# Layer 0's second product as two column tiles of 64 output rows each, in a two-layer graph attention kernel

## The chip, the cores and the metric

The kernel runs on one core of a Trainium2 chip. The metric is device time in microseconds (us) for one launch, which covers the whole computation for all 16 graphs. A core has a matrix engine (TensorE, PE in the profile; its weight loads are listed apart as PEld), VectorE (DVE), ScalarE (ACT), GpSimd (POOL) and queues that issue transfers (SP among them). The engines run beside each other and wait for each other's results.

## The reference, cut to what matters

Each of 16 graphs has 1024 nodes with 128 features, and a dense 0/1 adjacency matrix of 1024 x 1024. Everything is float32. Layer 0 is an attention layer with gates:

```python
h = jnp.einsum('bnf,df->bnd', x, Ww) + Wb
e = jnp.einsum('bjl,bkl->bjk', jnp.einsum('bjd,dl->bjl', h, A), h)
e = e + jnp.swapaxes(e, 1, 2)
scores = jnp.where(adj > 0, e, 0.0)
attention = jax.nn.softmax(scores, axis=1) * adj
h_prime = jax.nn.relu(jnp.einsum('bij,bjk->bik', attention, h))
...
return oc * jnp.tanh(ic * h_prime + fc * x)
```

Its output is added to x and normalised. Layer 1 has four heads, each with the two products `scores = h A h^T` and `tanh(adj * scores) @ h`; the heads' mean is added to its input and normalised again. The change concerns the product `attention @ h` of layer 0, which gives `h_prime`.

## The kernel before

Graphs are handled one after the other. For one graph the 1024 nodes are split into NB = 8 blocks of 128, and a row of 1024 results into NH = 2 ranges of 512 columns, the width of one matmul. The adjacency is held transposed, eight tiles of 128 x 1024 for a graph.

Layer 0 is a Python generator, `layer0(b)`. For each block j, `front(j)` makes the scores of block j against all nodes (line 232, two products into PSUM tiles `sc`), adds a bias and masks them on VectorE (line 235), takes the row maximum (line 240) and the exponential on ScalarE (line 242). `middle(j)` folds the softmax's denominator into the features, `hz = h / z` (lines 250 and 252), and multiplies by the adjacency (line 253). `back(j)` then adds the block's share to the accumulator `acc`: two products, one for each range of 512 columns, with `hz` (128 nodes x 128 features) as the stationary operand and `s` (128 nodes x 512) as the moving one (line 259). The accumulator is 128 features x 1024 nodes of PSUM and gathers the eight blocks; after the last one ScalarE turns it into `hpT` (line 276), which line 283 transposes for the gates.

In `layer0`, a step runs `front(i)`, yields, then runs `middle(i - 1)` and `back(i - 2)` and yields again, so a block is summed two steps after its scores.

The order of the work is written out by hand, and each engine runs its instructions in that order. The main loop at the end goes over 32 steps for a graph (4 heads x 8 blocks). A step issues `layer1_step`: the scores of one head and block (line 355, two products), their masking on VectorE (line 358) and tanh on ScalarE (line 362), and the second product of the step before the last (line 369, two products into layer 1's accumulator, lines 364 to 372). After that it advances the generator of the next graph's layer 0 by one piece. So a call of `back` stands in TensorE's order behind a pair of products of line 369 and before the next step's pair of line 355, or before line 175 (a head's projection) where one falls due. Layer 0 of the first graph has no layer 1 to run beside and runs ahead of the loop, with the preparation of the heads' weights (lines 114 to 131 and 141 to 147) between its pieces.

PSUM holds four shared tiles (`bank`) and the two accumulators `acc0` and `acc1`, which take the other half.

Of the kernel before, what the change touches and what calls it, by code (L numbers as in the profile page):

```python
# [22 lines left out]
def two_layer_adjacency_kernel(  # L23
# [26 lines left out]
    nc = tc.nc  # L50
    B, N, D = x.shape
    H = conv_w.shape[0]
    assert D == P and N % 512 == 0 and H % 2 == 0
    NB = N // P
# [143 lines left out]
    def layer0(b):  # L198
# [26 lines left out]
        acc = ps_acc.tile([P, N], F32, tag="acc0", name=f"acc0_{b}")  # L225
# [30 lines left out]
        def back(j):  # L256
            s, hz = steps.pop(j)
            for q in range(NH):
                nc.tensor.matmul(  # L259
                    acc[:, ts(q, 512)], hz, s[:, ts(q, 512)],  # L260
                    start=(j == 0), stop=(j == NB - 1),
                )

        for i in range(NB + 1):
            if i < NB:
                front(i)
                yield
            if i:
                middle(i - 1)
            if i > 1:  # L270
                back(i - 2)
            yield
        back(NB - 1)
        hpT = sb.tile([P, N], F32, tag="hpT", name=f"hpT_{b}", bufs=1)
        for q in range(NH):
# [209 lines left out]
```

## Time and profile before

| | us |
|---|---|
| median of the 2 runs shown | 2652.52 (2650.65 to 2654.38) |
| the profiled execution | 2653.64 |
| its span, first to last instruction | 2651.9 |
| TensorE busy | 2568.2 |
| VectorE busy | 1761.2 |
| ScalarE busy | 884.7 |
| GpSimd busy | 454.7 |

The profile is one execution, with times from the start of its span. A line of a group gives the source line, the engine and operation, the tiles written and read, the shape, and the count; behind it stand the busy time and the mean length of one in ns, and then the time for which the engine stood idle before such an instruction and what ended that. Matmuls overlap each other at their ends, so their mean length is longer than the step from one start to the next. In the slices, the span is cut into 40 equal parts and a digit is the busy share in tenths. A timeline line gives the start, the length, the engine, the instruction and how many were merged. The chain of waits follows the work back from the last instruction, at each step to whatever released it.

### The profile page before, as it was taken

What the parts mean: (1) busy time and instruction counts of PE and PEld (TensorE: products, weight loads), DVE (VectorE), ACT (ScalarE), POOL (GpSimd) and SP (SyncE); (2) the same over time, 40 slices, a digit from 0 to 9 for tenths busy, and PEclk for the clock granted to TensorE, in tenths of its full rate; (3) what the DMA queues carried; (4) which work ended last, traced back from release to release, by engine and by line L of the source; (5) the groups of instructions that cost most, each with busy time, mean ns of one, the idle gap of its engine ahead of it and who ended that gap; (6) DMA issues with size and microseconds to landing.
All of it is one profiled execution on the core that took longest, in us unless ns stands there. A gap on an engine that the chain in (4) does not pass through costs nothing.

```text
span 2651.9 us, 19837 instructions
## 1 busy us (share of the span) xinstructions
PE 2568.2 (97%) x6766; PEld 1229.0 (46%) x6766; DVE 1761.2 (66%) x3407; ACT 884.7 (33%) x1078; POOL 454.7 (17%) x200
## 2 busy tenths in 40 slices
PE   5699999999999999999999999999999999999997
PEld 3344444444444444444444444444444444444443
DVE  4566756767667576766767667576666767667554
ACT  1233333333333333333333333333333333333332
POOL 3121201212020121201212021121101212021000
PEclk7799999999999999999999999999999999999999
DMA  2202001020110102001020020101001020020000
GB/s 94 79 0 79 9 16 64 9 79 9 44 44 16 64 8 72 16 16 64 8 80 8 18 70 16 64 9 63 25 16 64 9 79 8 16 69 2 1 8 8
DMA packets 43526, 94.54 MB, mean 36 GB/s; under 512 B 4641, under 2 KB 22945, under 8 KB 43425
## 3 DMA queue, kind: packets, MB, share of 16 engines
q1 hardware_dynamic: 41120, 84.89, 9.1%
q0 software_dynamic: 2304, 8.39, 1.1%
q8 instruction: 53, 0.87, 0.1%
q14 instruction: 49, 0.39, 0.0%
HBM read 84.87 MB, written 8.39 MB: 35 GB/s over the span
## 4 chain that ended last, share of the span: by engine, by line
PE 90%; DVE 7%; issue 1%; ACT 1%; DMA 0%; SPq 0%; POOL 0%; POOLq 0%; ACTq 0%
PE acc L369 30%; PE sc L355 30%; PE acc L259 8%; PE sc L232 8%; PE pg L175 5%; PE pr L340 4%; DVE u L311 1%; DVE u L303 1%; DVE s L358 1%; PE pt L283 1%; PE pr L217 1%; DVE st L158 1%; DVE sum L381 1%; PE pt L393 1%; ACT x1T L327 0%
## 5 line engine op out<-in xcount | busy, mean ns | idle before, releaser
L358 DVE SCALAR_TENSOR_TENSOR s<-sc,h,adj 128x512 f32<-128x512 f32 x1024 | 746.3, 747 | 494.6 <-PE sc L355 472.3
L369 PE MATMUL acc<-s,h 128*128 128x512 f32 x2048 | 963.1, 593 | 14.7 <-DVE sum L381 14.7
L355 PE MATMUL sc<-x1T,g 128*128 128x512 f32 x2048 | 962.2, 592 | 0.0
L362 ACT ACTIVATE s<-s 128x1024 f32<-128x1024 f32 x512 | 541.1, 1057 | 1112.2 <-DVE s L358 1007.8
L369 PEld LDWEIGHTS acc<-s,h 128*128 128x128 f32 x2048 | 387.7, 190 | 509.5 <-issue 479.3
L355 PEld LDWEIGHTS sc<-x1T,g 128*128 128x128 f32 x2048 | 386.7, 190 | 434.8 <-issue 341.3
L207 POOL TENSOR_SCALAR mask<-adj 128x1024 bf16<-128x1024 f32 x128 | 354.4, 2780 | 364.3 <-DVE s L235 208.1
L242 ACT ACTIVATE s<-s,nmax 128x1024 f32<-128x1024 f32 x128 | 147.0, 1149 | 489.7 <-DVE nmax L240 472.1
L235 DVE SCALAR_TENSOR_TENSOR s<-sc,h,mask 128x512 f32<-128x512 f32 x256 | 186.0, 746 | 115.2 <-PE sc L232 101.8
L259 PE MATMUL acc<-s,hz 128*128 128x512 f32 x512 | 247.5, 607 | 2.3 <-DVE s L253 2.3
L232 PE MATMUL sc<-xT,gT 128*128 128x512 f32 x512 | 242.2, 596 | 0.0
L163 POOL TENSOR_TENSOR rs<-rs,mhalf 128x8 f32<-128x8 f32 x32 | 53.3, 1664 | 924.7 <-DVE rs L162 924.7
L299 POOL TENSOR_TENSOR u<-x,gate 128x1024 f32<-128x1024 f32 x16 | 30.5, 1908 | 863.3 <-DVE gate L297 808.1
L253 DVE TENSOR_TENSOR s<-s,adj 128x1024 f32<-128x1024 f32 x128 | 167.8, 1311 | 0.0
L240 DVE TENSOR_REDUCE nmax<-s 128x1 f32<-128x1024 f32 x128 | 156.2, 1220 | 4.4
L259 PEld LDWEIGHTS acc<-s,hz 128*128 128x128 f32 x512 | 99.0, 195 | 125.8 <-issue 117.7
L343 DVE TENSOR_TENSOR h<-pr,row_b 128x258 f32<-128x258 f32 x256 | 106.1, 425 | 74.1 <-PE pr L340 73.1
L232 PEld LDWEIGHTS sc<-xT,gT 128*128 128x128 f32 x512 | 97.4, 193 | 118.2 <-issue 113.1
L340 PE MATMUL pr<-row_w,x1T 128*128 128x258 f32 x512 | 127.7, 383 | 0.0
L175 PE MATMUL pg<-x1T,mT 128*128 128x512 f32 x256 | 123.6, 606 | 3.6 <-ACT x1T L327 3.6
L340 PEld LDWEIGHTS pr<-row_w,x1T 128*128 128x128 f32 x512 | 98.0, 191 | 55.1 <-issue 45.8
L176 ACT ACTIVATE g<-pg,tcol 128x512 f32<-128x512 f32 x128 | 87.8, 686 | 49.1 <-PE pg L175 46.8
(69 smaller groups left out, 909.8 us busy)
## 6 DMA issues: line engine op xcount, KB each, us to landing
adj<-in_adjT_dram SPq DMA_DIRECT2D x128, 512.0 KB, 4.4
xT<-in_xT_dram SPq DMA_DIRECT2D x16, 512.0 KB, 3.6
x<-in_x_dram SPq DMA_DIRECT2D x16, 512.0 KB, 4.0
out_dram<-y POOLq DMA_DIRECT2D x16, 512.0 KB, 3.9
row_w<-in_L_gnn_conv_w_dram SPq DMA_DIRECT2D x4, 64.0 KB, 2.9
wm<-in_L_gnn_attn_w_dram SPq DMA_DIRECT2D x4, 64.0 KB, 2.6
row_b<-in_L_gnn_conv_b_dram SPq DMA_DIRECT2D x4, 64.0 KB, 3.2
ct<-in_L_gnn_Ww_dram SPq DMA_DIRECT2D x1, 64.0 KB, 1.8
```

The costliest lines, as they stand in the source:

```text
L175: nc.tensor.matmul(pg, mT[i], src[:, ts(q, 512)], start=True, stop=True)
L207: nc.gpsimd.tensor_scalar(t, adj_t[b][j], 0.0, None, ALU.is_gt)
L232: nc.tensor.matmul(sc, gT[:, ts(j, P)], xTb[:, ts(q, 512)], start=True, stop=True)
L235: nc.vector.scalar_tensor_tensor(s[:, ts(q, 512)], sc, h[:, j, D : D + 1], masks[j][:, ts(q, 512)], op0=ALU.add, op1=ALU.mult,)
L240: nc.vector.tensor_reduce(nmax, s, AX.X, ALU.max, negate=True)
L253: nc.vector.tensor_mul(s, s, adj_t[b][j])
L259: nc.tensor.matmul(acc[:, ts(q, 512)], hz, s[:, ts(q, 512)], start=(j == 0), stop=(j == NB - 1),)
L340: nc.tensor.matmul(pr[:, :W1], x1T_t[b][:, ts(k, P)], row_w1[:, p, :], start=True, stop=True)
L355: nc.tensor.matmul(sc, g[:, ts(m, P)], x1T_t[b][:, ts(q, 512)], start=True, stop=True)
L358: nc.vector.scalar_tensor_tensor(s[:, ts(q, 512)], sc, rows[:, m, 2 * D + r : 2 * D + r + 1], adj[:, ts(q, 512)], op0=ALU.add, op1=ALU.mult,)
L362: nc.scalar.activation(s, s, AF.Tanh)
L369: nc.tensor.matmul(acc[:, ts(q, 512)], rows[:, m, ts(r, D)], s[:, ts(q, 512)], start=(m == 0), stop=(m == NB - 1),)
```

## The change

Each product of `back` is issued as two products. The first takes columns 0 to 63 of `hz` as the stationary operand and writes rows (partitions) 0 to 63 of `acc`; the second takes columns 64 to 127 and writes rows 64 to 127. Both read the same 512 columns of `s` whole. The sum over the eight blocks, the flags that open and close it, and every other line stay as they are. Line 232 and layer 1 still use the full width of the array.

```diff
         def back(j):
             s, hz = steps.pop(j)
             for q in range(NH):
-                nc.tensor.matmul(
-                    acc[:, ts(q, 512)], hz, s[:, ts(q, 512)],
-                    start=(j == 0), stop=(j == NB - 1),
-                )
+                for half in (slice(0, D // 2), slice(D // 2, D)):
+                    nc.tensor.matmul(
+                        acc[half, ts(q, 512)], hz[:, half], s[:, ts(q, 512)],
+                        start=(j == 0), stop=(j == NB - 1),
+                    )
```

## The prediction

> **What bounds the kernel now.** I read the page's busy times and slices first, then its chain of waits, the groups of section 5, and last the timeline and the chain around one call of the edited function.
>
> ```profile
> PE 2568.2 (97%) x6766; PEld 1229.0 (46%) x6766; DVE 1761.2 (66%) x3407; ACT 884.7 (33%) x1078; POOL 454.7 (17%) x200
> ...
> PE   5699999999999999999999999999999999999997
> ...
> PE 90%; DVE 7%; issue 1%; ACT 1%; DMA 0%; SPq 0%; POOL 0%; POOLq 0%; ACTq 0%
> ...
> L259 PE MATMUL acc<-s,hz 128*128 128x512 f32 x512 | 247.5, 607 | 2.3 <-DVE s L253 2.3
> ...
> L259 PEld LDWEIGHTS acc<-s,hz 128*128 128x128 f32 x512 | 99.0, 195 | 125.8 <-issue 117.7
> ```
>
> TensorE is full from the third slice to the last but one, and 90% of the chain is TensorE's: what is added there is added to the time. L259, the edited line, waited 2.3 us in all, so there is no slack to put work into. The code asks for 16 batches x 8 blocks x 2 column ranges = 256 products there and the row counts 512: each float32 product is two weight loads and two matmuls ("passes" below).
>
> A busy matmul may hide its true rate, so I take that from the chain of waits about 1.48 ms in:
>
> ```profile
> 1481.79 1.72 PE acc L259 x4
> 1483.51 1.72 PE sc L355 x4
> 1485.23 1.72 PE acc L369 x4
> 1486.94 1.72 PE sc L232 x4
> 1488.66 1.72 PE sc L355 x4
> ```
>
> and the timeline of TensorE:
>
> ```profile
> 1500.51 1.88 PE L369 MATMUL acc<-s,h 128*128 128x512 f32 x4
> 1502.23 1.88 PE L259 MATMUL acc<-s,hz 128*128 128x512 f32 x4
> 1503.95 1.88 PE L175 MATMUL pg<-x1T,mT 128*128 128x512 f32 x4
> ```
>
> Four passes, whatever the line, take 1.72 us from start to start: a **slot** of 0.43 us each. A pass lasts 0.592 us by itself (median of line L259), so its last 0.162 us lies beside the next pass. The loads:
>
> ```profile
> 1502.23 0.19 PEld L259 LDWEIGHTS acc<-s,hz 128*128 128x128 f32 x1 [0.24 <-issue]
> 1502.66 0.19 PEld L259 LDWEIGHTS acc<-s,hz 128*128 128x128 f32 x1 [0.24 <-issue]
> ```
>
> The load for the next pass begins as a pass begins and takes 0.19 us: one load ahead, hidden, with 0.24 us to spare.
>
> **What the Trainium skill says.** "TensorE: Matmul & The Clock Gate", Part 3 (packing small matmuls), says that matmuls with outputs at different column groups run together in one array: three column tiles of 32 columns gained 2.38x. The same section says that matmuls start and end strictly in program order; the timelines here agree (every pass starts after the one before). "TensorEngine Tiling (Array Packing)", Key Properties, says that tiles work independently, but a change of tiling mode drains TensorE. Every weight load in this trace is 128 columns wide, so no run here shows a tile running beside another, or a drain. "FP8 and Floating Point Precision", TensorE Precision Notes, says that true float32 takes four passes through the array; the trace shows two matmuls of 0.43 us for 512 columns, 0.84 ns a column and matmul.
>
> **The change part by part.** Per call of `back` four passes of 128 columns become eight of 64 over the same 512 moving columns; nothing else is added. Calls: 16 x 8 = 128; slots added if nothing runs beside anything: 4.
>
> (1) *Do the halves run beside each other?* Call the lower tile A and the upper B. Program order is A1 A2 B1 B2, then the same for the second column range (primes). If starts stay in order and a tile does one pass at a time, A2 waits for A1, B1 may start with A2, and so on: slot one A1, two A2 and B1, three B2 and A1', four A2' and B1', five B2'. That is five slots where four were: only the second pass of a half lies beside the first pass of the other. Price: 1 x 0.43 x 128 = **55.0 us**. Bounds: 0 (all pairs together) and 4 x 0.43 x 128 = **219.9 us** (nothing together).
>
> (2) *Change of mode.* Each call lies between full-width matmuls (L369 before it, L355 or L175 after it in the lines above), so there are two changes a call, 256 in all. No trace row shows one. A drain as such costs the tail, 0.592 - 0.430 = 0.162 us; if the next load cannot run ahead either, its exposed part is added. I price that at 0.08 us: where TensorE restarts from a stop, four passes take 1.80 us to the next start (1529.27 - 1527.47) instead of 1.72:
>
> ```profile
> 1527.47 1.96 PE L369 MATMUL acc<-s,h 128*128 128x512 f32 x4 [0.98 <-DVE sum L381]
> 1529.27 1.02 PE L355 MATMUL sc<-x1T,g 128*128 128x512 f32 x2
> ```
>
> So a change costs at most 0.24 us and at least nothing (the tail may lie beside the next mode's first pass; a gain is excluded, as the order of starts stays): 0 to 62 us in all. I take the middle, 0.12 us, or **31 us**.
>
> (3) *Loads inside a call.* With the one-deep lead of the trace, B1's load starts only as A2 starts, and B1 comes late by what is exposed; the same for A1' and B1': three per call. Bounds 0 and 0.19 us (the whole load), 0 to 73 us; at half the exposed 0.08 us of the restart it is 3 x 0.04 x 128 = **15 us**. Nothing below zero: the load of 64 columns may be shorter, but it was hidden before.
>
> (4) *The first batch.* Its 8 calls (38 to 90 us) are counted in the 128. They run at a lower granted clock; at 38.07 us the four passes take 3.55 us to the next start, so a slot there is up to twice as dear, at most 8 x 0.43 = 3.4 us more for one extra slot and 14 us for four. Waits of TensorE on other engines there (8.5 us on DVE s, 18.1 us on ct at L118) follow in program order and would hide little. I take 0.
>
> (5) *Costed at nothing.* The activation of acc into hpT waits for the last call of a batch, and comes about a microsecond later. After that call at 1502.23 TensorE has L175, L355 and L369 until L283 at 1509.10; hpT was done at 1505.24, 3.9 us before it is read. If that cover went, L283 would wait, up to 16 times. Buffers of s and hz come free later by a microsecond, while VectorE (66% busy) and GpSimd (17%) have room. No semaphore, transfer or queue is added; SP's and POOL's queues stay as they were.
>
> Sum of the likeliest case: 55 + 31 + 15 = 101 us. The profiled execution took 2653.6 us (span 2651.9 and 1.7 around it), 1.1 us over the median shown. 2653.6 + 101 = about **2755 us**, 3.8% slower. This case's own range: 2709 (one slot, nothing else) to 2653.6 + 55 + 62 + 31 (load exposed at 0.08) = 2802.
>
> **Rivals.** *The tiles don't run beside each other*: the change then does not do what column tiles are for. For it: float32 passes take twice the cycles a column would need, and no trace here shows two passes streaming together. Against it: the skill's measured 2.38x, with a type it does not name. Time: 2653.6 + 219.9 = 2873 without drains, to 2936 with 62 us of them. It decides if start-to-start inside a call stays at 0.43 us.
>
> *No loss (the other side)*: A and B stream together on both passes. The place is the queue of L259, the price 0 extra slots; it decides if B1 starts within a few nanoseconds of A1, which needs the passes to be interleaved A1 B1 A2 B2, or each product's two passes to be held by its own tile rather than by the queue. Left are the changes of mode, 0 to 62 us, likely under the bare tail's 2 x 0.162 x 128 = 41 us: 2654 to 2695, within 2%. For it: tiles are said to be independent. Against it: starts in program order.
>
> *Faster* has hardly a mechanism: the work of a tile is the old number of slots, and what became cheaper (loads) was hidden. Only the first batch, where TensorE waits at restarts, could gain a few tenths of a microsecond.
>
> **Numbers.** Overlap with one slot lost 0.51; serial 0.36; no loss 0.12; anything faster by over 2%, 0.01. A change of 2% (53 us, limits 2599.5 and 2705.6) is about what a measurement of this kernel tells from none. Both of the large cases lie above the limit; the third lies below it, and I give the lower edge of the first 0.01 more: faster 0.01, same 0.13, slower 0.86. The range 2700 to 2915 holds the first case and all of the serial case but its dearest drains (0.05); with the no-loss case left out below, some 0.18 is outside. The gap between 2802 and 2873 belongs to an overlap with dearer loads.
>
> **What would show it.** L259 with 1024 matmuls and loads of 128x64; in the timeline, starts within a call: pairs about together and 2.1 to 2.5 us per call from start to the next line's start (one slot lost), 3.4 us or more (serial), 1.7 to 2.0 (no loss). The mode change shows as a longer step from the last L369 pass to the first of L259, and again behind it, than 0.43 us. L355, L369 and L232 should keep 1.72 us for four. The prediction is wrong if those lines change, if the step into a call exceeds 0.7 us, or if VectorE or an hpT wait takes a share of the chain that it did not have.

## The result, and the profile after

| | before | after |
|---|---|---|
| median, us | 2652.52 (2650.65 to 2654.38) | 2695.74 (2695.13 to 2696.35) |
| the profiled execution, us | 2653.64 | 2696.35 |
| its span, us | 2651.9 | 2694.6 |

The ratio is 1.0165, with an interval of 1.014 to 1.0189: slower by 43 us, or 1.6%. That is within 2% and clear of the spread of the runs. It was forecast to be slower by 101 us, and the measured time lies 4 us below the lower end of the forecast's range. Of the executions below, two ran at a lower granted clock, 0.921 and 0.571 against 0.987, and took longer (2816.2 us with all products in tiles, 7740.6 us with pairs of blocks at full width); they are left out of medians and ratios.

The edit shifts the lines below it by one: L259 is now L260, L355 is L356 and L369 is L370. The page of the kernel after, in the order of the lines shown of before:

```profile
PE 2610.1 (97%) x7278; PEld 1182.1 (44%) x7278; DVE 1761.2 (65%) x3407; ACT 885.8 (33%) x1078; POOL 454.5 (17%) x200
...
PE 90%; DVE 7%; issue 1%; ACT 1%; DMA 0%; SPq 0%; POOL 0%; POOLq 0%; ACTq 0%
...
L260 PE MATMUL acc<-s,hz 128*64 128x512 f32 x1024 | 254.2, 618 | 2.1 <-DVE s L253 2.1
...
L260 PEld LDWEIGHTS acc<-s,hz 128*64 128x64 f32 x1024 | 63.3, 138 | 171.9 <-issue 156.2
```

TensorE ran 512 more matmuls, as expected, but its busy time grew by 42 us only, and that of the edited line by 7 us (254.2 against 247.5). Twice the passes took hardly more busy time on their own line. Busy times of passes that overlap don't say where the time went; the chain of waits of the kernel after does (start, length, line, number of passes):

```profile
1504.69 1.72 PE acc L370 x4
1506.40 1.87 PE acc L260 x8
1508.27 1.91 PE sc L356 x4
1510.19 1.72 PE acc L370 x4
```

Eight passes of the edited line take 1.87 us where four took 1.72: no slot of 0.43 us was lost. The four passes behind them, which the edit doesn't touch, take 1.91 instead of 1.72. The sum of both is 0.34 us a call. In the 120 calls behind the first graph's, 60 are followed by line 356, 30 by line 175 and 30 by line 341 (the heads' rows), all at full width, so each of them has two changes between full width and tiles (changes of mode below). The timeline of TensorE, asked for short stretches of one such call, shows the single steps. First the entry:

```profile
1505.81 0.59 PE L370 MATMUL acc<-s,h 128*128 128x512 f32 x1
1506.34 0.65 PE L260 MATMUL acc<-s,hz 128*64 128x512 f32 x2
```

then the exit:

```profile
1507.67 0.60 PE L260 MATMUL acc<-s,hz 128*64 128x512 f32 x2
1508.20 1.55 PE L356 MATMUL sc<-x1T,g 128*128 128x512 f32 x3
```

and the weight loads of the same call:

```profile
1506.33 0.20 PEld L260 LDWEIGHTS acc<-s,hz 128*64 128x64 f32 x4 [0.76 <-issue]
1506.82 0.14 PEld L260 LDWEIGHTS acc<-s,hz 128*64 128x64 f32 x2 [0.28 <-issue]
1507.25 0.14 PEld L260 LDWEIGHTS acc<-s,hz 128*64 128x64 f32 x2 [0.29 <-issue]
1508.20 0.30 PEld L356 LDWEIGHTS sc<-x1T,g 128*128 128x128 f32 x2 [0.81 <-DVE s L253]
1508.74 0.19 PEld L356 LDWEIGHTS sc<-x1T,g 128*128 128x128 f32 x1 [0.24 <-issue]
```

The line with two passes in 0.65 us is the point: a pass alone lasts about that long, so two run together from the start of the call (their starts lie under 0.01 us apart in the trace). The step from the last full-width pass into the call is 0.53 us by these lines (1506.34 - 1505.81), a tenth more than a slot. The loads for the call stand at 1506.33, not a slot ahead as at full width. The first pair takes 0.48 us (1506.34 to 1506.82, where the loads beside the second pair start), 0.05 too long, the later ones 0.43. On the way out the step is again 0.53 us, and the first full-width pass takes 0.54 (1508.20 to 1508.74). Over those 120 calls the medians of the four are 0.52, 0.48, 0.52 and 0.53 us. So a call costs 0.09 + 0.05 on the way in and 0.09 + 0.10 on the way out, with 0.01 for the later start of the second tile about 0.35 us. In the first graph the delay is smaller: hpT begins 1.0 us later (91.0 against 90.0 us). 120 calls x 0.35 + 1.0 = 43 us, against 42.7 us between the two spans.

### The profile page after: what moved, and what is told of

Its sections match the earlier page's. It is cut to its first block, busy times and chain, and to the rows that moved or that the text cites. A ratio compares the mean times of both kernels' runs of the same rounds, so it can differ in the third digit from the quotient of the medians.

```text
span 2694.6 us, 20861 instructions
## 1 busy us (share of the span) xinstructions
PE 2610.1 (97%) x7278; PEld 1182.1 (44%) x7278; DVE 1761.2 (65%) x3407; ACT 885.8 (33%) x1078; POOL 454.5 (17%) x200
## 4 chain that ended last, share of the span: by engine, by line
PE 90%; DVE 7%; issue 1%; ACT 1%; DMA 0%; SPq 0%; POOL 0%; POOLq 0%; ACTq 0%
PE sc L356 30%; PE acc L370 30%; PE acc L260 9%; PE sc L232 8%; PE pg L175 5%; PE pr L341 4%; DVE u L312 1%; DVE u L304 1%; DVE s L359 1%; PE pt L284 1%; PE pr L217 1%; DVE st L158 1%; DVE sum L382 1%; PE pt L394 1%; ACT x1T L328 0%
## 5 line engine op out<-in xcount | busy, mean ns | idle before, releaser
L370 PE MATMUL acc<-s,h 128*128 128x512 f32 x2048 | 963.2, 593 | 14.6 <-DVE sum L382 14.6
L356 PE MATMUL sc<-x1T,g 128*128 128x512 f32 x2048 | 968.5, 595 | 0.0
L370 PEld LDWEIGHTS acc<-s,h 128*128 128x128 f32 x2048 | 387.7, 190 | 509.5 <-issue 479.3
L356 PEld LDWEIGHTS sc<-x1T,g 128*128 128x128 f32 x2048 | 381.7, 190 | 454.7 <-issue 324.8
L260 PE MATMUL acc<-s,hz 128*64 128x512 f32 x1024 | 254.2, 618 | 2.1 <-DVE s L253 2.1
L260 PEld LDWEIGHTS acc<-s,hz 128*64 128x64 f32 x1024 | 63.3, 138 | 171.9 <-issue 156.2
```

The lines of the kernel that those rows point to most:

```text
L260: nc.tensor.matmul(acc[half, ts(q, 512)], hz[:, half], s[:, ts(q, 512)], start=(j == 0), stop=(j == NB - 1),)
L356: nc.tensor.matmul(sc, g[:, ts(m, P)], x1T_t[b][:, ts(q, 512)], start=True, stop=True)
L370: nc.tensor.matmul(acc[:, ts(q, 512)], rows[:, m, ts(r, D)], s[:, ts(q, 512)], start=(m == 0), stop=(m == NB - 1),)
```

## The experiments

Two things had to be told apart. Is the loss a price for each **stretch** of tiled passes (two changes of mode), or for each tiled product? And why was no slot lost: how can B1 start beside A1 when A2 stands ahead of it? Times are medians, each beside the kernel before on the same chip (2652.0 to 2653.2 us). Each edit is shown against the changed kernel, unless the text names another.

| run | us | ratio to before, interval |
|---|---|---|
| halves outermost | 2696.3 | 1.0163 (1.0148 to 1.0178) |
| one range of two | 2697.8 | 1.0168 (1.0153 to 1.0183) |
| four tiles of 32 | 2693.9 | 1.0154 (1.0139 to 1.0169) |
| layer 1 as well | 2817.8 | 1.0621 (1.0603 to 1.0638) |
| all products | 2659.4 | 1.0026 (1.0015 to 1.0037) |
| pairs of blocks, full width | 2652.0 | 1.0001 (0.9993 to 1.001) |
| pairs of blocks, tiles | 2674.5 | 1.0084 (1.0071 to 1.0098) |
| pairs of blocks, halves outermost | 2784.4 | 1.0497 (1.0482 to 1.0511) |
| four tiles, quarters outermost | 2697.1 | 1.0169 (1.0152 to 1.0186) |

### Halves outermost: does a waiting pass hold up the other tile?

```diff
-            for q in range(NH):
-                for half in (slice(0, D // 2), slice(D // 2, D)):
+            for half in (slice(0, D // 2), slice(D // 2, D)):
+                for q in range(NH):
```

> The same eight passes a call, but both column ranges of the lower tile are asked for before those of the upper one. If a pass that waits for its own tile doesn't hold up a pass of the other tile, the upper tile's passes still run beside the lower one's: four slots a call, 43 us over the kernel before, about 2696 us. If starts keep the order of the program, the lower tile's four passes come first and only the last lies beside the upper tile's first: seven slots, 3 x 0.43 x 128 = 165 us more, about 2861 us. If a product's two passes are merely swapped with its neighbour's before they reach the queue, neighbours are now in one tile and the result is again near 2861 us.

2696.3 us: the time of the change. The loads of one call:

```profile
1504.82 0.20 PEld L260 LDWEIGHTS acc<-s,hz 128*64 128x64 f32 x4 [0.76 <-issue]
1505.30 0.15 PEld L260 LDWEIGHTS acc<-s,hz 128*64 128x64 f32 x2 [0.28 <-issue]
```

Four loads at once and then two a slot, as in the change, and the call's eight passes still took four slots. Each tile has four passes to do, and a tile alone starts one a slot (that is shown under "How far can a pass start ahead?"). So the first upper pass ran in the first slot, with three lower passes ahead of it in the program that could not yet have started. A strict order of starts falls with this run, and so does a swap of neighbours. What is said ahead of the prediction, that each engine runs its instructions in the order in which they are written, does not hold for the starts of TensorE's tiled passes.

### One range of two

```diff
-                for half in (slice(0, D // 2), slice(D // 2, D)):
+                for half in ((slice(0, D),), (slice(0, D // 2), slice(D // 2, D)))[q]:
```

> Only the second range of 512 columns is split into two tiles; the first stays at full width. There are still two changes of mode a call, but half the tiled products. If the loss is the changes alone, it stays at 43 us: about 2696 us. If it belongs to the tiled products (a late second tile, exposed loads between them), it halves: about 2674 us.

2697.8 us, 44.6 over before, with half of the tiled products: the loss stayed whole. It is the changes, not the tiled work between them.

### Four tiles of 32

```diff
-                for half in (slice(0, D // 2), slice(D // 2, D)):
+                for half in [ts(c, D // 4) for c in range(4)]:
```

> Four tiles of 32 columns in place of two of 64: sixteen passes a call. If all tiles run together and the loss is a drain plus an exposed first load in proportion to its columns (0.05 us for 64, 0.106 us for 128 in the trace of the change), the entry gets 0.026 us cheaper and the exit stays: 128 x 0.026 = 3 us less, about 2692 us. If only two tiles can run together, four more slots a call, 4 x 0.43 x 128 = 220 us on top, about 2916 us. If the loss grows with the number of passes, above 2730 us.

2693.9 us, 2.4 us under the halves outermost, measured beside it, where 3.3 us under the change was expected (128 x 0.026). The chain of waits of this run:

```profile
1504.34 1.72 PE acc L370 x4
1506.06 1.85 PE acc L260 x16
1507.91 1.91 PE sc L356 x4
```

Sixteen passes in the place of four, and they take 1.85 us. The median first step of a call is 0.45 us, 0.03 less than with 64 columns: this agrees with a first load that is exposed in proportion to its columns. About half of that gain is lost again, as the fourth tile starts 0.02 us behind the first. The step out of the call and the one behind it are the same as with 64. The gain in the median is about as large as the spread of the runs, so the steps in the trace carry this more than the times do.

### Layer 1's second product as well

```diff
             for q in range(NH):
-                nc.tensor.matmul(
-                    acc[:, ts(q, 512)], rows[:, m, ts(r, D)], s[:, ts(q, 512)],
-                    start=(m == 0), stop=(m == NB - 1),
-                )
+                for c in range(2):
+                    nc.tensor.matmul(
+                        acc[ts(c, D // 2), ts(q, 512)], rows[:, m, ts(2 * r + c, D // 2)],
+                        s[:, ts(q, 512)], start=(m == 0), stop=(m == NB - 1),
+                    )
```

> Layer 1's second product is split into two column tiles as well, the edit of back kept. A step then has one stretch of tiled passes, with layer 0's products joined to it without a change between: 512 stretches beside the loop's steps and 8 in the first graph alone. If the loss is a price for each stretch (0.34 us), 520 x 0.34 = 177 us, about 2829 us. If it is a price for each call of a tiled product pair, 640 x 0.34 = 218 us, about 2870 us. If it belonged to layer 0's line alone, about 2696 us.

2817.8 us, 164.7 over before: nearest to a price for each stretch (177), and 12 us under it. Most of that is in TensorE's waits. This is a row of the kernel after (us in total, times, longest):

```profile
PE acc L370 <- DVE sum L382: 14.6, 15, 1.0
```

and this the same wait here:

```profile
PE acc L371 <- DVE sum L383: 4.2, 15, 0.3
```

A later TensorE finds VectorE done, and 10.4 us of waiting went. 177 - 10 = 167 is within 3 us of the measured loss; a price for each call, less the same 10 us, would be 208.

### All products, so that hardly a change of mode is left

The edit is shown against the kernel before, for one of the eight lines with a product. Every product of both layers goes through this helper, that of line 283 too; the transposes of lines 326 and 393 and the preparation of the weights stay as they were.

```diff
+    def mm(out, lhsT, rhs, start=True, stop=True):
+        for c in range(2):
+            nc.tensor.matmul(
+                out[ts(c, P // 2)], lhsT[:, ts(c, P // 2)], rhs, start=start, stop=stop
+            )
...
-                nc.tensor.matmul(
-                    sc, gT[:, ts(j, P)], xTb[:, ts(q, 512)], start=True, stop=True
-                )
+                mm(sc, gT[:, ts(j, P)], xTb[:, ts(q, 512)])
```

> Every product of both layers is issued as two column tiles of 64; only the transposes and the preparation of the weights stay at full width. If the loss is the changes of mode, nearly all of it goes: what is left is the two groups of transposes of each graph, 32 stretches x 0.34 us = 11 us, about 2664 us. If a tiled product costs something of its own (0.34 us for two products, 2680 products of 512 columns or fewer), the loss grows to several hundred us, above 3000 us.

2659.4 us: with over ten times the tiled passes, the loss fell from 43 to 7 us, where 11 were expected. The kernel was run again for its trace:

> The kernel with every product of both layers in tiles once more, for its trace: four lower and four upper passes of a pair of products in four slots, 1.72 us from start to start on every line as in the kernel before, and longer steps at the transposes alone; about 2660 us.

2658.5 us, in one execution. The timeline of TensorE, where line 116 is the helper's:

```profile
1503.50 1.89 PE L116 MATMUL acc<-s,hz 128*64 128x512 f32 x8
1505.21 1.89 PE L116 MATMUL pg<-x1T,mT 128*64 128x512 f32 x8
1506.93 1.89 PE L116 MATMUL sc<-x1T,g 128*64 128x512 f32 x8
1508.65 1.89 PE L116 MATMUL acc<-s,h 128*64 128x512 f32 x8
```

Eight passes of 64 columns take 1.72 us from start to start, as four of 128 did before, on the edited line and on all others. Tiled work itself costs nothing here, and gains nothing either. Nearly all of the 7 us are those of the transposes: from the four slots before such a group to the four behind it, line 393 takes 4.61 us for 4.31 in the kernel before, and line 326 takes 4.94 for 4.81. That is 0.30 and 0.13 us, for 16 graphs 6.9 us. Behind line 326 TensorE waits 0.24 us for ScalarE in both kernels, and there the way out adds nothing.

### Two blocks at a time: the price halved

The control is the kernel before, with the products of two blocks together:

```diff
-            if i > 1:
-                back(i - 2)
+            if i > 1 and i % 2:
+                back(i - 3)
+                back(i - 2)
             yield
+        back(NB - 2)
         back(NB - 1)
```

with four buffers for s instead of three, and 17 for the adjacency instead of 18.

> The control of the next two runs: full width as before the change, but the products of two blocks are issued together, four times a graph, with one more buffer for s and one less for the adjacency. Every theory expects the time before, about 2653 us, unless the buffers or the new order cost something of their own.

2652.0 us: order and buffers cost nothing. The same edit on the changed kernel:

> The same order and buffers as the control, with the column tiles of 64: 64 tiled stretches with 16 passes each in place of 128 with 8. If the loss is a price for each stretch, it halves: 64 x 0.34 = 22 us over the control. If it is a price for each product, it stays at 43 us over the control.

2674.5 us, 22.5 over the control: half of the loss with half of the stretches and the same number of tiled passes. Of the versions that leave other lines at full width this is the cheapest; none was faster than the kernel before.

### How far can a pass start ahead?

The next edit is shown against the run before, the pairs of blocks in tiles:

```diff
-        def back(j):
-            s, hz = steps.pop(j)
-            for q in range(NH):
-                for half in (slice(0, D // 2), slice(D // 2, D)):
+        def back(*js):
+            for half in (slice(0, D // 2), slice(D // 2, D)):
+                for j in js:
+                    s, hz = steps[j]
+                    for q in range(NH):
...
-                back(i - 3)
-                back(i - 2)
+                back(i - 3, i - 2)
```

> As the run before, but all lower halves of the two blocks (eight passes) stand ahead of all upper halves. If the queue can start an upper pass past seven waiting lower ones, the time is that of the run before, 22 us over the control. If it looks past only three (as many as in the run with the halves reordered in one call), the upper tile starts four slots late: 4 x 0.43 x 64 = 110 us more. If it doesn't look past at all, 7 x 0.43 x 64 = 193 us more.

2784.4 us, 110 over the run before: four slots a pair of blocks were lost. The weight loads of one such pair of blocks:

```profile
1516.97 0.19 PEld L261 LDWEIGHTS acc<-s,hz 128*64 128x64 f32 x2 [0.76 <-issue]
1517.45 0.14 PEld L261 LDWEIGHTS acc<-s,hz 128*64 128x64 f32 x1 [0.29 <-issue]
1517.88 0.14 PEld L261 LDWEIGHTS acc<-s,hz 128*64 128x64 f32 x1 [0.29 <-issue]
1518.31 0.14 PEld L261 LDWEIGHTS acc<-s,hz 128*64 128x64 f32 x1 [0.29 <-issue]
1518.74 0.19 PEld L261 LDWEIGHTS acc<-s,hz 128*64 128x64 f32 x3 [0.29 <-issue]
1519.17 0.19 PEld L261 LDWEIGHTS acc<-s,hz 128*64 128x64 f32 x2 [0.24 <-issue]
```

After the two loads at the start there is one a slot, the lower tile's, and one pass starts in each of the first four slots. So a pass of 64 columns takes a slot, as one of 128 does, and the eight passes in four slots of the earlier runs can't have been eight shorter ones in a row. At 1518.74, as the fifth lower pass starts and the last three of the eight wait, the upper tile's loads join. Two readings were left: three waiting passes in all, or three for each tile. The edit that tells them apart, against the four tiles of 32:

```diff
-            for q in range(NH):
-                for half in [ts(c, D // 4) for c in range(4)]:
+            for half in [ts(c, D // 4) for c in range(4)]:
+                for q in range(NH):
```

> Four tiles of 32 columns, as before, but a tile's four passes stand together: first tile, second, third, fourth. The theory made from the paired run is that a pass may start while at most three earlier passes, counted over all tiles, still wait. Worked through slot by slot, the third tile then starts in the third slot and the fourth in the fourth, and a call takes seven slots for four: 3 x 0.43 x 128 = 165 us over the quarters in the other order, about 2859 us. If the three are counted for each tile apart, nothing is lost: about 2694 us. If starts were strictly in order, thirteen slots and about 3189 us.

2697.1 us. The theory that I took into this run, three in all, fell: 165 us did not come. The fourth tile's first pass ran in the first slot with nine passes ahead that waited, three for each of the other tiles. The 3 us over the other order are mostly the stagger of the tiles: here the fourth starts 0.04 us behind the first, there 0.02, and 128 x 0.02 = 2.6 us. The loads of one call:

```profile
1506.27 0.18 PEld L260 LDWEIGHTS acc<-s,hz 128*32 128x32 f32 x8 [0.76 <-issue]
1506.72 0.15 PEld L260 LDWEIGHTS acc<-s,hz 128*32 128x32 f32 x4 [0.28 <-issue]
```

Eight loads at once at the start, two for each of four tiles. What fits all runs is that TensorE deals passes out in order, to a short queue of each tile: one that runs and three that wait. A fifth pass for a tile waits at the head and holds up whatever stands behind it, whichever tile that is for. That is a model that fits, not a thing seen: the trace doesn't say which tile a record belongs to. Counts of five to seven passes for a tile were not run, so the four rests on the slot in which the upper loads began and on these two orders.

## Why the prediction was wrong

The step that failed is **(1)**, the five slots: "If starts stay in order and a tile does one pass at a time, A2 waits for A1, B1 may start with A2". Its second condition holds (a tile does one pass at a time); its first, that starts stay in order, doesn't. The Trainium skill, "TensorE: Matmul & The Clock Gate", Part 3, says that matmuls start and end strictly in program order, and I let that order decide. The full-width timelines that seemed to agree could not have shown otherwise: with one tile, order and occupancy are the same thing. The runs differ from the page, and the measurement decides: in the run with the halves outermost upper passes start ahead of three lower ones. The 55 us of this step were 0: a call takes 1.87 us, four slots and a change, not five slots. The speedup of column tiles that the same page gives pointed the right way.

The rival that I gave 0.12, **no loss**, is what happened, for the second of the two reasons named there: passes are held by their own tile rather than by the queue. Its time, 2654 to 2695, ended just below the measured 2695.7, because it priced the changes at the bare tail, 41 us, where 43 came. Of the signs named, the 1.7 to 2.0 us a call came; line 356 behind a call did not keep its 1.72 us for four passes (1.91), as part of the price of leaving the tiles falls on it.

Step **(2)**, the changes of mode, was right in kind. It was sized at the middle of its bounds, 0.12 us, and is about 0.17 us a change: 43 us and not 31. (There are 252 changes, not 256: the last three calls of the first graph stand together in the trace.) "TensorEngine Tiling (Array Packing)", Key Properties, says that such a change drains TensorE. The step of 0.52 us both ways shows a wait of 0.09 us before the new mode, less than the 0.162 us of the tail that I had as the drain. The rest is the longer first step behind a change, by 0.05 us with loads of 64 columns and 0.10 with 128, which I read as the exposed first load; I had taken 0.08 from a restart for both.

Step **(3)**, exposed loads inside a call, was priced at 15 us and is 0: from the second pair on, passes follow at 0.43 us, as each tile's next load goes ahead beside its running pass. That steps (2) and (3) together gave 46 us against 43 measured is a coincidence of one too small and one too large.

Step **(4)** held in its size: the first graph ended 1.0 us later, where its six stretches at 0.35 us would be 2.1. Why it was less isn't shown. TensorE's waits there hardly shrank (that for VectorE's s at the edited line from 2.3 to 2.1 us), and at the changing clock single calls differ both ways: to the next line's start the first took 3.35 us for 3.55 before, the second 3.61 for 3.40. Step **(5)** held. ScalarE's wait for acc grew from 26.9 to 29.3 us, and TensorE's wait for hpT stayed at 0.7 us.

The serial rival, 0.36, is excluded by two passes in 0.65 us and by 1.87 us a call. The range was set so that it left out the no-loss case, and it was that case's upper end that came.

## What to carry to other kernels

In these runs column tiles of one mode ran beside each other in float32, and splitting a full-width product into them cost nothing as such; what cost time was each change between tiled and full-width passes, about 0.17 us, part of it on the neighbours' lines. So put tiled products together, or tile the neighbours as well. Four passes in a row for one tile cost nothing here and eight did, so give the tiles their passes in turn. Where a step of a forecast rests on an order that the trace at hand cannot show broken, the case in which the order doesn't hold belongs in the range.

## What the runs showed of the hardware

- A pass for one column tile started ahead of passes for other tiles that stood earlier in the program: past three waiting ones with two tiles and nine with four. With eight in a row for one tile, the other tile started only when three were left waiting (110 us lost over 64 pairs of blocks, four slots each).
- Sixteen passes of 32 columns ran in the time of four of 128 but for the entry: 1.85 us against 1.72.
- A change between full width and tiles took 0.09 us more than a slot before the first pass of the new mode. The first step behind it was longer than a slot by 0.05 us with loads of 64 columns, 0.02 with 32 and 0.10 with 128.
- With every product in tiles, eight passes of 64 columns took 1.72 us from start to start, as four of 128 did.
